# One more GpSimd DRAIN ahead of the last unit's scatter-adds in a mixture-of-experts layer

## The chip, the cores and the metric

The kernel runs on one core of a Trainium2 chip. The metric is the device time of one execution in microseconds (us), the median of several executions. A profile of one execution gives what each engine did: TensorE (PE, with its weight loads as PEld), VectorE (DVE), ScalarE (ACT), GpSimd (POOL) and SyncE (SP), and the 16 DMA engines.

## What is computed

A mixture-of-experts layer with a residual. 4096 tokens (64 x 64) of 256 values are normed and gated; each takes its two best of 8 experts. An expert is three dense layers, 256 to 512 to 512 to 256. The two results are weighted with the gate's values and added to the token's row.

```python
xn = rms_w * (x * jax.lax.rsqrt(var + EPS))
gate = xn @ wg_W + wg_b + (genre_embed @ gg_W + gg_b)
topk_w, topk_i = jax.lax.top_k(jax.nn.softmax(gate, axis=-1), TOP_K)
cw = jnp.sum(jax.nn.one_hot(topk_i, E) * topk_w[..., None], axis=-2)
h1 = jax.nn.relu(jnp.einsum('bsh,ehm->bsem', x, W1) + b1)
h2 = jax.nn.relu(jnp.einsum('bsem,emn->bsen', h1, W2) + b2)
out_e = jnp.einsum('bsen,enh->bseh', h2, W3) + b3
out = x + jnp.einsum('bseh,bse->bsh', out_e, cw)
```

The reference computes every expert for every token; the kernel computes only the two chosen ones.

## The kernel before

The kernel first gates all tokens and builds lists of tokens by expert, in tiles of 128 tokens. Tiles of one expert that follow each other form a unit of one to four tiles. The first 8 units (one tile for each expert) run while the rest of the routing is still computed. The other units come from a plan. How many of them there are, and how wide, depends on the data, so the program holds 40 plans, each as a branch of its own (a `Switch` at L1449); one of them runs. The units' order within a branch is fixed when the kernel is built: every engine gets its instructions in the order of the text.

For a unit, GpSimd gathers the tokens' rows and gate values with indirect DMAs (L844), SyncE passes the rows through a scratch in DRAM to turn them, ScalarE's queue brings the expert's weights, and TensorE does the three layers. In `step_fast` (L1296) the first two layers of a unit of two to four tiles are done by a scheme of seven products instead of eight (`Fast`); VectorE forms the sums. The third layer of a unit is done in the step of the unit behind it: `layer3(u - 1)` (L1147) and then `give(u - 1)` (L1156).

`give` is where a result leaves. For each tile VectorE forms `y` from the products in PSUM, the gate's weight and the bias (L1167), and GpSimd issues a scatter-add (L1168): an indirect DMA that adds the 128 rows of `y` to the tokens' rows of the output in DRAM. A token appears in two experts' units, and a row is read, added to and written back; so the scatter-adds of a unit wait until those of the unit before it have landed. Within a unit no token appears twice, and its scatter-adds don't wait for each other.

The steps of a branch are issued by `steps` (L1395), whose last argument, `last`, is the number of the plan's units and the head's 8. The step of unit `last - 1` is that of the last unit: it issues its first two layers and the scatter-adds of unit `last - 2`. One more step, `u == last`, issues the third layer of the last unit, tile by tile, and its scatter-adds (L1285 to L1289). Behind it the program ends: SyncE waits until all transfers have landed, every engine has a DRAIN, and all meet at a barrier. These instructions carry the line L1484.

In the run shown the last units have two tiles each. `steps` is also called with one unit at a time ahead of the branch (L1445); there `last` is far off.

Of the kernel before, what the change touches and what calls it, by code (L numbers as in the profile page):

```python
# [52 lines left out]
def kernel(  # L53
# [17 lines left out]
    nc = tc.nc  # L71
# [741 lines left out]
    def width(u):  # L813
        return BT if u < E else SQ * plan[u - E][1]

    def size(u):
        return (width(u) + BT - 1) // BT

    def paired(u):
        return size(u) > 1  # L820
# [49 lines left out]
    def gather_cw(u):  # L870
        for k, b in enumerate(tiles(u)):
            cg = cgs[b] = cgR[:, turn_of(u, k) % NCG]
            fetch(cg, (cwdA if b < E else cwdR)[:, :], b)
# [14 lines left out]
    def shuffle(u):  # L888

        nc.sync.dma_start(  # L890
            shs[:, slots(u)].rearrange("p s k f -> p s (k f)"),
            passing(u).rearrange("(s g) (b k) f -> (g b) s (k f)", g=P // SQ, b=SQ),
        )

    def transpose_x(u):
        bs, w, s0 = tiles(u), len(tiles(u)), slots(u).start
        if u > E:
            for k in range(w):
                V.transpose(  # L899
                    xT[:, :, s0 + k, :].rearrange("p c (b k) -> p k c b", b=SQ),  # L900
                    shs[:, s0 + k].rearrange("p k (a c) -> p k c a", a=SQ),
                )
            return
        if u < E:
            tps = [PB[4][:, c * BT : (c + 1) * BT] for c in range(HC)]
        else:
            tps = [PB[4], PB[7]]
        for c in range(HC):
            for k, b in enumerate(bs):
                g = ring(run, [P, H], "xg", 3, b) if u < E else xgR[u % 2][:, k]  # L910
                nc.tensor.transpose(tps[c][:, ts(k, BT)], g.rearrange("p (r c) -> p c r", c=HC)[:, c], ident)  # L911
            if u == E:
                (nc.scalar.copy if c else V.tensor_copy)(
                    xT[:, c, slots(u), :], tps[c].rearrange("p (s t) -> p s t", s=w)
                )
        if u < E:
            nc.scalar.copy(xT[:, :, s0, :], PB[4][:, 0 : HC * BT].rearrange("p (c t) -> p c t", c=HC))
# [35 lines left out]
    def stream_1(u, engine=mybir.EngineType.Activation):  # L953
        e = expert(u, engine)
        QUEUES[engine].dma_start(w1r[u % RING], W1[e].rearrange("e (p c) m -> p (e c) m", c=HC))

    def stream_3(u, engine=mybir.EngineType.Activation):
        e = expert(u, engine)
        QUEUES[engine].dma_start(w3r[u % RING], W3[e].rearrange("e (c p) h -> p (e c) h", p=P))

    def streams(u, end):
        if E < u + 2 < end:
            stream_1(u + 2)
        if E < u + 1 < end:
            stream_3(u + 1)

    def stage_1(u):

        if u < E:
            ww[u] = [w1r[u % RING], vT[:, :, u, :], w2a[:, u], w3r[u % RING]]  # L970
            return
        e = ex[u] = expert(u, mybir.EngineType.DVE)
        bb = ring(run, [P, 2, MC], "bb", 3, u)
        V.tensor_copy(bb.unsqueeze(2), vT[:, :, e])
        ww[u] = [w1r[u % RING], bb, st2, w3r[u % RING]]

    def stage_2(u):
        if u >= E:
            V.tensor_copy(st2, w2a[:, ex[u]].rearrange("p e c m -> p (e c) m"))

    def scales(u):

        for k, b in enumerate(tiles(u)):
            cw = ring(run, [P, 1], "cw", 8, turn_of(u, k))
            V.tensor_copy(cw, cgs[b][:, ex[u]])
            cgs[b] = cw

    def scaled(u, eng="V"):

        cws = []  # L990
        e = expert(u, mybir.EngineType.Activation) if eng == "A" and u >= E else ex.get(u)
        for k, b in enumerate(tiles(u)):
            cg = cgs.pop(b)
            bc = ring(run, [P, H], "bc", 4, turn_of(u, k))
            if u < E:
                cw, b3e = cg[:, u : u + 1], b3_sb[:, u, :]
            else:
                cw, b3e = cg, b3_sb[:, e].rearrange("p e h -> p (e h)")
            if eng == "V":
                V.tensor_scalar(bc, b3e, cw, None, ALU.mult)  # L1000
            else:
                nc.scalar.mul(bc, b3e, cw)
            cws.append((cw, bc))
        ex.pop(u, None)
        ww[u].append(cws)

    def layer1(u):
        w1, bb = ww[u][0:2]
        w = width(u)
        cols = xT[:, :, slots(u), :].rearrange("p c s t -> p c (s t)")  # L1010
        for m in range(MC):
            ph = PB[m][:, 0:w]
            for c in range(HC):
                nc.tensor.matmul(  # L1014
                    ph, lhsT=w1[:, c, ts(m, P)], rhs=cols[:, c, :], start=(c == 0), stop=(c == HC - 1)
                )
            nc.scalar.activation(hid[0][:, m, 0:w], ph, AF.Relu, bias=bb[:, 0, m : m + 1])

    def layer2(u, between=None):
        _, bb, w2 = ww[u][0:3]  # L1020
        for n in range(MC):
            ph = PB[n][:, 2 * BT : 3 * BT]
            for m in range(MC):
                nc.tensor.matmul(  # L1024
                    ph, lhsT=w2[:, m, ts(n, P)], rhs=hid[0][:, m, 0:BT], start=(m == 0), stop=(m == MC - 1)
                )
            nc.scalar.activation(hid[1][:, n, 0:BT], ph, AF.Relu, bias=bb[:, 1, n : n + 1])
            if between and n in between:
                between[n]()
# [117 lines left out]
    def layer3(u, which=None, order=range(MC)):  # L1147
        w3 = ww[u][3]
        for k in which or range(size(u)):
            for i, n in enumerate(order):  # L1150
                cols = within(u, k)
                nc.tensor.matmul(  # L1152
                    sums(u, k)[0 : cols.stop - cols.start], lhsT=hid[1][:, n, cols], rhs=w3[:, n, :], start=(i == 0), stop=(i == MC - 1)
                )
# [104 lines left out]
    def fetches_of(u, last):  # L1259
        far = E + 1 < u + 2 < last  # L1260
        if far:
            gather_unit(u + 2)
            stow(u + 2)
        return far

    def step(u, last):

        far = fetches_of(u, last)
        if u < last:
            layer1(u)  # L1270
            if u >= E:
                streams(u, last)
            stage_2(u)
        if u + 1 < last:
            gather_cw(u + 1)
        if u - 1 >= E:
            scales(u - 1)
        scaled(u - 1)
        if u + 1 < last:
            stage_1(u + 1)  # L1280
            if u + 1 > E:
                transpose_x(u + 1)
        if far:
            shuffle(u + 2)
        if u == last:  # L1285
            for k in reversed(range(size(u - 1))):
                layer3(u - 1, [k], (2, 3, 0, 1) if 2 * k * BT >= width(u - 1) else range(MC))
                give(u - 1, [k])
            return  # L1289
        layer3(u - 1)  # L1290
        if u == E - 1:
            stream_1(E + 2, mybir.EngineType.SP)
            stream_3(E + 1, mybir.EngineType.SP)
        give(u - 1)
# [100 lines left out]
    def steps(u0, u1, last):  # L1395
        for u in range(u0, u1):
            if u < last and paired(u):
                step_fast(u, last)
                continue
            step(u, last)  # L1400
            if u < last:
                layer2(u)

    CUT = E + NQT - 2
    ENGS = (
# [7 lines left out]
    with tc.manual_schedule():  # L1413
# [21 lines left out]
        for u in range(E - 1, CUT):  # L1435
            if u == CUT - 2:
                _, (arm,) = nc.values_load_multi_w_load_instructions(
                    nex[0:1, 0:1],
                    min_val=0,
                    max_val=len(ARMS) - 1,  # L1440
                    skip_runtime_bounds_check_because="the number of a shape of the tail",
                )
            elif u == CUT - 1:
                tc.switch_hint({e: arm for e in ENGS}, len(ARMS), "tail")
            steps(u, u + 1, E + NQT + 1)  # L1445
# [3 lines left out]
    for k in tc.Switch(arm, len(ARMS), hint="tail"):  # L1449
        for d, old in zip(kept, state):  # L1450
            d.clear()
            d.update({b: list(v) if isinstance(v, list) else v for b, v in old.items()})
        adds[:] = [list(a) for a in done]
        plan[:] = ARMS[k]
        last = E + len(plan)
        with tc.manual_schedule():
            steps(CUT, last + 1, last)
# [31 lines left out]
```

## Time and profile before

| what | us |
|---|---|
| median of 3 runs (465.6 to 468.07) | 467.16 |
| the profiled execution | 467.09 |
| its span, first to last instruction | 465.4 |
| TensorE busy | 450.8 (97%) |
| VectorE busy | 334.2 (72%) |
| GpSimd busy | 265.1 (57%) |
| ScalarE busy | 217.6 (47%) |
| transfers generated by GpSimd, share of 16 DMA engines | 22.2% |
| mean granted TensorE clock | 0.992 |

"Busy" counts the work of an engine and leaves out instructions that only steer it: moves of registers, branches, waits for semaphores and DRAINs. Such instructions appear in the views under a name with a q behind it (POOLq, SPq). An indirect DMA on GpSimd is busy while GpSimd generates its descriptors, and its data lands later. In the view in order of time a bracket gives how long the engine stood idle before the instruction and what ended that.

### The profile page before, as it was taken

How to read it: one execution, taken by the hardware profiler on the slowest of the kernel's cores; microseconds unless marked ns; L12 is line 12 of the kernel's file. 1: busy time of each engine (PE TensorE's matmuls, PEld its weight loads, DVE VectorE, ACT ScalarE, POOL GpSimd, SP SyncE). 2: the span in 40 equal slices, each digit the busy share in tenths (PEclk: the TensorE clock that was granted, in tenths of full speed). 3: DMA queues.
4: the chain of work that ended last, by engine and by line, in shares of the span. 5: the costliest groups of instructions: out<-in, count | busy, mean ns of one | idle time of the engine just before them, and what ended most of it. 6: DMA issues, size and time to landing. Idle time of an engine off the chain costs nothing.

```text
span 465.4 us, 8614 instructions
## 1 busy us (share of the span) xinstructions
PE 450.8 (97%) x2750; PEld 407.3 (88%) x2750; DVE 334.2 (72%) x889; ACT 217.6 (47%) x511; POOL 265.1 (57%) x231
## 2 busy tenths in 40 slices
PE   7899999999999999999999999999999999999991
PEld 5689999968888888888899999899999889999991
DVE  5787896266758576675867576777877887898850
ACT  4746443435344262526362625264464455555550
POOL 4255532757877878384746464757646545564222
PEclk9999999999999999999999999999999999999996
DMA  8699999793866766564636464655656664665322
GB/s 293 241 290 375 376 369 377 265 260 83 228 127 172 141 169 131 137 115 114 128 86 140 90 143 112 140 145 108 143 146 125 153 160 109 162 155 137 70 25 25
DMA packets 75629, 78.74 MB, mean 169 GB/s; under 512 B 34927, under 2 KB 64082, under 8 KB 75188
## 3 DMA queue, kind: packets, MB, share of 16 engines
q1 hardware_dynamic: 48976, 43.29, 30.1%
q0 software_dynamic: 14960, 17.47, 22.2%
q10 hardware_dynamic: 11636, 17.32, 11.3%
q8 instruction: 24, 0.39, 0.3%
q14 instruction: 33, 0.27, 0.2%
HBM read 62.60 MB, written 20.12 MB: 178 GB/s over the span
## 4 chain that ended last, share of the span: by engine, by line
PE 89%; issue 4%; DMA 3%; DVE 1%; POOL 1%; ACT 0%; ACTq 0%; DVEq 0%; POOLq 0%
PE pb L1105 50%; PE pb L1152 24%; PE pb L1024 6%; PE pb L1014 5%; DMA out_dram<-y,idxR 2%; PE pb L247 1%; POOL out_dram L1168 1%; PE pb L604 1%; PE pb L278 1%; DMA gTs<-in_L_cond_rms_w_dram 1%; PE pb L911 1%; DMA xg<-in_x_dram,idxA 1%; PE pb L284 0%; PE pb L539 0%; DVE hid L1123 0%
## 5 line engine op out<-in xcount | busy, mean ns | idle before, releaser
L1168 POOL DMA_INDIRECT out_dram<-y,idxR x59 | 95.4, 1618 | 105.0 <-DVE y L1167 52.4
L1152 PE MATMUL pb<-w3r,hid 128*128 128x256 f32 (+3 forms) x536 | 125.6, 380 | 0.0
L1152 PEld LDWEIGHTS pb<-w3r,hid 128*128 128x128 f32 (+3 forms) x536 | 96.9, 186 | 14.4 <-DVE y L1167 0.4
L1126 ACT ACTIVATE hid<-hid,bb 128x256 f32<-128x256 f32 (+13 forms) x148 | 70.2, 523 | 34.2 <-DVE hid L1123 30.2
L1105 PE MATMUL pb<-hid,big 128*128 128x256 f32 (+7 forms) x456 | 83.4, 326 | 0.0
L1105 PEld LDWEIGHTS pb<-hid,big 128*128 128x128 f32 x456 | 71.9, 191 | 5.9 <-issue 1.4
L844 POOL DMA_INDIRECT cg<-cwdR,idxR x59 | 63.9, 1083 | 18.0 <-issue 17.7
L1114 ACT COPY q1s<-pb 128x256 f32<-128x256 f32 (+7 forms) x54 | 25.3, 469 | 69.8 <-PE pb L1105 69.5
L1114 ACT COPY big<-pb 128x512 f32<-128x512 f32 (+7 forms) x57 | 27.2, 476 | 65.9 <-PE pb L1105 65.9
L1105 PE MATMUL pb<-mixB,big 128*128 128x256 f32 (+7 forms) x304 | 55.5, 326 | 0.1
L1105 PE MATMUL pb<-hotA,big 128*128 128x256 f32 (+7 forms) x304 | 52.3, 325 | 0.0
L1105 PEld LDWEIGHTS pb<-mixB,big 128*128 128x128 f32 x304 | 47.8, 191 | 3.1 <-DVE hid L1123 0.5
L1105 PEld LDWEIGHTS pb<-hotA,big 128*128 128x128 f32 x304 | 47.3, 191 | 2.7
L844 POOL DMA_INDIRECT xgE<-in_x_dram,idxR x31 | 33.5, 1082 | 17.3 <-issue 15.7
L1105 PE MATMUL pb<-mixX,iotx 128*128 128x128 f32 (+7 forms) x216 | 43.1, 322 | 0.0
L1105 PEld LDWEIGHTS pb<-mixX,iotx 128*128 128x128 f32 x216 | 35.5, 191 | 2.4
L844 POOL DMA_INDIRECT big<-in_x_dram,idxR x28 | 30.4, 1084 | 8.5 <-issue 7.0
L1167 DVE SCALAR_TENSOR_TENSOR y<-pb,cw,bc 128x256 f32<-128x256 f32 (+3 forms) x59 | 27.5, 479 | 7.7 <-PE pb L1152 7.2
L1126 ACT ACTIVATE hid<-pb,bb 128x128 f32<-128x128 f32 (+7 forms) x74 | 26.6, 411 | 12.4 <-PE pb L1105 12.1
L1024 PEld LDWEIGHTS pb<-hid,w2a 128*128 128x128 f32 x256 | 29.8, 192 | 1.1 <-issue 0.8
L1024 PE MATMUL pb<-hid,w2a 128*128 128x128 f32 x256 | 30.5, 276 | 0.0
L899 DVE STREAM_TRANSPOSE xT<-gTs 128x256 f32<-128x256 f32 x55 | 29.1, 638 | 0.0
(300 smaller groups left out, 643.1 us busy)
## 6 DMA issues: line engine op xcount, KB each, us to landing
w3r<-in_L_cond_W_dram ACTq DMA_DIRECT2D x17, 512.0 KB, 5.0
w2a<-in_L_cond_W_dram SPq DMA_DIRECT2D x8, 1024.0 KB, 13.3
w1r<-in_L_cond_W_dram ACTq DMA_DIRECT2D x16, 512.0 KB, 3.7
w1r<-in_L_cond_W_dram SPq DMA_DIRECT2D x11, 512.0 KB, 11.4
w3r<-in_L_cond_W_dram SPq DMA_DIRECT2D x10, 512.0 KB, 13.5
gTs<-scr SPq DMA_DIRECT2D x7, 512.0 KB, 4.2
out_dram<-in_x_dram SPq DMA_DIRECT2D x4, 768.0 KB, 9.3
big<-in_x_dram SPq DMA_DIRECT2D x4, 512.0 KB, 5.0
```

Source lines behind the costliest of these rows:

```text
L247: nc.tensor.transpose(TB[bank][:, ts(k, P)], xin[j][:, k, ts(c, P)], ident)
L278: nc.tensor.matmul(bank[r : r + 32, :], lhsT=wg_sb[:, c, :], rhs=turned(n), start=True, stop=True)
L844: return nc.gpsimd.indirect_dma_start(out=dst, out_offset=None, in_=src, in_offset=bass.IndirectOffsetOnAxis(ap=index(b), axis=0), bounds_ ...
L899: V.transpose(xT[:, :, s0 + k, :].rearrange("p c (b k) -> p k c b", b=SQ), shs[:, s0 + k].rearrange("p k (a c) -> p k c a", a=SQ),)
L1014: nc.tensor.matmul(ph, lhsT=w1[:, c, ts(m, P)], rhs=cols[:, c, :], start=(c == 0), stop=(c == HC - 1))
L1024: nc.tensor.matmul(ph, lhsT=w2[:, m, ts(n, P)], rhs=hid[0][:, m, 0:BT], start=(m == 0), stop=(m == MC - 1))
L1105: nc.tensor.matmul(bank[:, ts(n, self.w)], lhsT=w[:, c, ts(n, P)], rhs=x[:, c], start=new and n == 0 and c == 0, stop=n == HB - 1 and c == ...
L1114: nc.scalar.copy(self.q[(1, 6, 5).index(k)], self.tall(self.X if k == 5 else self.U))
L1126: nc.scalar.activation(out, src, AF.Relu, bias=ww[self.u][1][:, self.l, n : n + 1])
L1152: nc.tensor.matmul(sums(u, k)[0 : cols.stop - cols.start], lhsT=hid[1][:, n, cols], rhs=w3[:, n, :], start=(i == 0), stop=(i == MC - 1))
L1167: V.scalar_tensor_tensor(y[0:n], sums(u, k)[0:n], cw[0:n], bc[0:n], ALU.mult, ALU.add)
L1168: add = nc.gpsimd.indirect_dma_start(out=orows, out_offset=bass.IndirectOffsetOnAxis(ap=index(b)[0:n], axis=0), in_=y[0:n], in_offset=None ...
```

## The change

The loop of `steps` is written without its `continue`, and behind the step of unit `last - 1` GpSimd gets a DRAIN: an instruction that holds the engine's queue until the engine has finished what was issued before. It names no tile and waits for no semaphore. It stands behind the scatter-adds of unit `last - 2` and ahead of those of unit `last - 1`. Each of the 40 branches has one; of these one runs. The calls ahead of the branch never reach `u == last - 1`. Otherwise each engine's instructions and waits are the same and in the same order. Lines behind the edit are higher by two.

```diff
         for u in range(u0, u1):
             if u < last and paired(u):
                 step_fast(u, last)
-                continue
-            step(u, last)
-            if u < last:
-                layer2(u)
+            else:
+                step(u, last)
+                if u < last:
+                    layer2(u)
+            if u == last - 1:
+                nc.gpsimd.drain()
```

## The prediction

> **What bounds the kernel now.** I read the page from the top down and then went to its end, because the one added instruction can touch the end alone.
>
> ```profile
> span 465.4 us, 8614 instructions
> ...
> PE 450.8 (97%) x2750; PEld 407.3 (88%) x2750; DVE 334.2 (72%) x889; ACT 217.6 (47%) x511; POOL 265.1 (57%) x231
> ...
> L1168 POOL DMA_INDIRECT out_dram<-y,idxR x59 | 95.4, 1618 | 105.0 <-DVE y L1167 52.4
> ```
>
> TensorE is busy for 97% of the span, so it sets the pace up to its last matmul, shortly before 456 us. GpSimd (POOL) is not a bound in the middle: its scatter-adds stand 105 us idle, mostly waiting for VectorE's `y`. What lies behind TensorE's last matmul is a path of its own, and there a microsecond is a microsecond. The view in order of time, GpSimd's rows of its end:
>
> ```profile
> 445.40 1.55 POOL L1168 DMA_INDIRECT out_dram<-y,idxR  x1 [9.16 <-DVE y L1167]
> ...
> 447.26 1.55 POOL L1168 DMA_INDIRECT out_dram<-y,idxR  x1 [0.31 <-issue]
> ...
> 454.87 1.55 POOL L1168 DMA_INDIRECT out_dram<-y,idxR  x1 [6.06 <-DVE y L1167]
> ...
> 456.72 1.55 POOL L1168 DMA_INDIRECT out_dram<-y,idxR  x1 [0.30 <-issue]
> ```
>
> The first two are the scatter-adds of the last unit but one, issued in the step of the last unit; the other two are the last unit's own. The new DRAIN stands between the second and the third. There GpSimd does nothing from 447.26 + 1.55 = 448.81 to 454.87, which is the 6.06 us in the bracket.
>
> The page stops at 458.27 and the span at 465.4. Those 7.1 us are filled by instructions that it does not count as busy. The view of one source line shows them; L1484 is the end of the program (the four upper rows from the stretch 457.2 to 464.6, the last from 464.6 on; columns: minimum, median and maximum in ns, first and last start):
>
> ```profile
> L1484 SPq EVENT_SEMAPHORE  x10: 28/28/28, 458.8 to 460.9; - x10
> L1484 SPq DRAIN  x2: 7/10/13, 460.9 to 461.0; - x2
> L1484 POOLq DRAIN  x1: 7722/7722/7722, 456.8 to 456.8; - x1
> L1484 POOLq EVENT_SEMAPHORE  x1: 17/17/17, 464.6 to 464.6; - x1
> ...
> L1484 POOLq DRAIN  x2: 46/83/120, 464.7 to 465.1; - x2
> ```
>
> SyncE has seen every transfer land and stands at the barrier at 461.0. GpSimd reaches it only at 464.6, because its own DRAIN runs from 456.80 for 7.72 us, to 464.52. Every other engine's DRAIN is over by then. So the last 3.5 us of the path are GpSimd's DRAIN alone: 464.56 (the semaphore behind it) less 461.06 (SyncE's second DRAIN at 461.01, and 0.05 for the semaphore).
>
> How much of the 7.72 is waiting? The last scatter-add ends on GpSimd at 456.72 + 1.55 = 458.28, so 6.24 us come after it. In the chain of waits the second scatter-add lands 3.73 us after its start:
>
> ```profile
> 447.26 3.73 DMA out_dram<-y,idxR
> 450.98 0.03 issue
> 451.01 0.04 POOLq L1168
> ```
>
> By that the last one lands at 456.72 + 3.73 = 460.45, which agrees with SyncE's last waits at 458.8 to 460.9. The DRAIN goes on for 4.07 us after the last byte has landed. It is therefore not the landing alone that it waits for. The other DRAINs of the same engine are short:
>
> ```profile
> L1475 POOLq DRAIN  x1: 183/183/183, 0.4 to 0.4; - x1
> ```
>
> 183 ns at the start, before any transfer of GpSimd's, and 120 and 46 ns directly behind the long one. The long one is the first DRAIN behind all the transfers that GpSimd generates: 59 + 59 + 31 + 28 + 8 + 8 + 8 = 201 indirect ones by the groups of its engine, and 7 plain ones.
>
> **The change, part by part.** One DRAIN with no semaphore of its own, on one engine, in the branch of the program that runs. The order of all other instructions and their waits is the same. No transfer is added or moved, so SyncE's and ScalarE's queues see nothing. Queued behind it are only the wait for the two earlier scatter-adds (451.0) and the last unit's two scatter-adds; nobody but the end of the program waits for those. The rewritten `continue` is host code.
>
> *Price of the new DRAIN.* Before has no DRAIN in the middle. From below: 46 ns, the shortest of GpSimd's; from above 7.72 us, the whole long row, counted from 448.81. The nearest row is the long one, since it too stands behind some 200 transfers: 6.24 us after the scatter-add before it, or 6.24 x 206/208 = 6.18 if it goes by the number of transfers. I take 6.18: 448.81 + 6.18 = 454.99.
>
> *What is late next.* Behind the long DRAIN the next semaphore instruction came 0.04 us later, and a scatter-add that waits for nothing starts 0.30 us behind its predecessor (the bracket at 456.72). So the third scatter-add starts at 454.99 + 0.34 = 455.33 instead of 454.87: 0.46 us late. The fourth follows its predecessor and is as late: 457.18, ending at 458.74 and landing at 460.91. SyncE is at the barrier at 461.06 + 0.46 = 461.52.
>
> *Price of the last DRAIN.* From above: 6.24 us after 458.74, as before. From below: 0.05 us, as for the ones directly behind a DRAIN. If its length is what has piled up since the last DRAIN, two transfers are left of 208, 6.24 x 2/208 = 0.06 us, and even if it must also see them land it is over at about 460.95, before SyncE's 461.52. I take this.
>
> *Sum.* The barrier then falls to SyncE at 461.52 instead of GpSimd at 464.56: 3.04 us less. Against the profiled execution's own 467.09 us (span 465.36 and 1.73 around it) that is 464.05; the median of the runs shown, 467.16, is 0.07 above it: 464.1 us. The cover for the new DRAIN is the 6.06 us in which GpSimd waits for `y`; without it the DRAIN would cost its whole 6.2 and the change would lose about 3.
>
> The Trainium skill speaks against this. "VectorE: DVE Perf Modes", section "The DRAIN you can't avoid", says that the DRAINs of the program's start and end take about 12 ns, constantly, on all five engines. SyncE's rows (7 to 13 ns) agree and GpSimd's 7722 ns does not; by the page's price the new DRAIN would be free, the last one would have nothing to give, and the time would be 467.2. "Perfetto Trace Analysis", section "DMA Instruction — SWDGE (GPSIMD)", says that the profiled end of such a transfer is the end of descriptor generation, not of the data's movement. The 3.73 us to landing against 1.55 agree; if the DRAIN waited for movement alone, the last one would have ended near 460.5 and bounded nothing.
>
> **The rivals.**
>
> *Every DRAIN with a transfer behind the previous one pays the same* (a fixed round of questions to the 16 DMA engines, say). For it: the trace has just one such DRAIN, and the three short ones had no new transfer, so rows alone cannot separate "since the last DRAIN" from "any at all". Against it: 4.07 us after landing is long for a question whose answer is known. Then the new one ends at 448.81 + 6.24 = 455.05, or, counted from landing, 450.98 + 4.07 = 455.05 as well. The scatter-adds are 0.52 late and the last DRAIN adds its full 6.24: +0.5, 467.7 us. It begins to lose where the new DRAIN passes 454.87 - 0.34 - 448.81 = 5.72 us.
>
> *The long row belongs to the end of the program* and a DRAIN elsewhere takes 46 to 183 ns. Then it disappears in the gap and the time stays 467.2. For it: the line is the program's end, which holds more than this instruction. Against it: two other GpSimd DRAINs of the same line are short.
>
> *Slower: the new DRAIN is stretched by work beside it, and the last keeps its length.* The place is 448.9 to 454.8, where by the view of stretches VectorE is busy 2.47 us and ScalarE 2.44 of 5.90, while both are at 0.00 behind 458.3. The price goes by GpSimd's scatter-adds: 1552 ns at the quiet end, 2102 at the worst, a factor of 1.35. 6.24 x 1.35 = 8.4 us ends at 457.2, the scatter-adds are 2.7 late: 469.8 us. It passes 0.5% from a DRAIN of 5.72 + 2.34 = 8.06 us on. Against it: the median scatter-add, 1624, is only 1.05 times the quiet one, which gives 6.5 us and +0.8.
>
> **How the numbers follow.** What a measurement of this kernel can tell from no change is about 0.5%, 2.34 us: faster means under 464.8, slower over 469.5. The forecast gets 0.55. Its own range is 463.5 (the new DRAIN nearly free: 3.5 us less) to 465.2 (the new one somewhat longer than taken, or a last one that keeps half its 6.24, to 461.9, which leaves 2.7; with both about 2). I put 0.49 of the 0.55 under 464.8. The same price for every DRAIN gets 0.27, no effect 0.11, both within 0.5%; the stretched DRAIN gets 0.07, with 0.06 of it over 469.5. Faster 0.49, same 0.45, slower 0.06. The range for 8 in 10 has to hold most of the forecast and the two cases near 467: 463.4 to 468.0.
>
> **What would show it.** A GpSimd DRAIN of 5.5 to 6.5 us behind 448.8; the third scatter-add 0.3 to 0.6 us later than 454.87; the DRAIN at the end well under 3 us after its last scatter-add; and the barrier released by SyncE near 461.5. If the last DRAIN is again some 6 us, the first rival is right. If the one in the middle is under 0.2 and the last unchanged, it is the second. A DRAIN over 8 us in the middle is the third. The rows up to 448.8 should not differ at all; a difference there would be something that I have not seen.

## The result, and the profile after

| | before | changed |
|---|---|---|
| median of 22 runs each, us | 466.63 (465.17 to 470.26) | 464.39 (462.85 to 468.91) |
| ratio of the changed to before, 95% interval | | 0.9949 [0.9929, 0.9968] |
| the profiled execution, us | 467.09 | 463.89 |
| its span, us | 465.4 | 462.1 |

The change is 2.24 us faster by the medians, half a per cent, and the interval excludes no change. Here and below a ratio compares only the faster executions of the two kernels and a median takes all of them, so a ratio is not the quotient of two medians. The page of the changed kernel shows almost nothing of it:

```profile
span 462.1 us, 8615 instructions
...
PE 449.9 (97%) x2750; PEld 407.2 (88%) x2750; DVE 334.4 (72%) x889; ACT 217.5 (47%) x511; POOL 265.2 (57%) x231
...
L1168 POOL DMA_INDIRECT out_dram<-y,idxR x59 | 95.3, 1615 | 106.0 <-DVE y L1167 46.4
```

One instruction more, and every engine as busy as before to within 0.9 us. Only the idle time ahead of the scatter-adds has another cause in part: 46.4 us are put down to `y` instead of 52.4. The view in order of time says where. GpSimd's last four scatter-adds:

```profile
444.44 1.55 POOL L1168 DMA_INDIRECT out_dram<-y,idxR  x1 [9.16 <-DVE y L1167]
446.29 1.55 POOL L1168 DMA_INDIRECT out_dram<-y,idxR  x1 [0.30 <-issue]
455.01 1.55 POOL L1168 DMA_INDIRECT out_dram<-y,idxR  x1 [7.17 <-issue]
456.87 1.55 POOL L1168 DMA_INDIRECT out_dram<-y,idxR  x1 [0.31 <-issue]
```

The bracket of the third was 6.06 us, ended by `y`. Now it is 7.17, and `y` does not end it. VectorE's row for that `y`, before and then changed:

```profile
454.11 0.48 DVE L1167 SCALAR_TENSOR_TENSOR y<-pb,cw,bc 128x256 f32<-128x256 f32 x1 [1.49 <-PE pb L1152]
...
453.15 0.48 DVE L1167 SCALAR_TENSOR_TENSOR y<-pb,cw,bc 128x256 f32<-128x256 f32 x1 [1.49 <-PE pb L1152]
```

In the changed kernel it ends at 453.63, and the scatter-add starts 1.38 us later; before, it started 0.28 us after its `y` (454.59 to 454.87). So the DRAIN made it 1.10 us late. The views of the two lines L1404 (the new DRAIN) and L1486 (the end of the program, L1484 before), the latter from 455.5 to 461.3; columns are minimum, median and maximum in ns, then first and last start:

```profile
L1404 POOLq DRAIN  x1: 8894/8894/8894, 445.2 to 445.2; - x1
```

```profile
L1486 SPq EVENT_SEMAPHORE  x10: 28/28/28, 458.8 to 461.1; - x10
L1486 SPq DRAIN  x2: 7/10/13, 461.2 to 461.2; - x2
...
L1486 POOLq DRAIN  x1: 4893/4893/4893, 455.8 to 455.8; - x1
L1486 POOLq EVENT_SEMAPHORE  x1: 17/17/17, 461.3 to 461.3; - x1
```

The new DRAIN's row begins at 445.25, before the second scatter-add ahead of it has even started (446.29), so its length says little by itself; it has to be counted from that transfer's end. The new one lasts until 454.14, which is 6.30 us behind the end of the second scatter-add (447.85). The one at the end of the program ends at 460.73: 2.30 us behind the last scatter-add instead of 6.24. GpSimd is then at the barrier before SyncE, whose second DRAIN is at 461.2.

To compare executions, I count from the end of the third `y`, the last thing ahead of GpSimd's path, in the same trace:

| us after the third `y`'s end | before | changed |
|---|---|---|
| third scatter-add starts | 0.28 | 1.38 |
| fourth scatter-add ends | 3.69 | 4.79 |
| GpSimd's last long DRAIN ends | 9.93 | 7.10 |
| SyncE stands at the barrier | 6.42 | 7.61 |
| the span ends | 10.77 | 8.44 |

The tail, from the end of the third `y` to the end of the span, is 2.33 us shorter. The spans differ by 3.3 because `y` itself was 0.96 us earlier in this execution (453.63 against 454.59). The DRAIN cannot have caused that: the rows ahead of it were early already (the first scatter-add above at 444.44 instead of 445.40), and the medians' 2.24 us agree with the tail.

### The profile page after: what moved, and what is told of

Same layout as the page of the kernel before. It is cut to its first block, busy times and chain, and to the rows that moved or that the text cites. A ratio compares the mean times of both kernels' runs of the same rounds, so it can differ in the third digit from the quotient of the medians.

```text
span 462.1 us, 8615 instructions
## 1 busy us (share of the span) xinstructions
PE 449.9 (97%) x2750; PEld 407.2 (88%) x2750; DVE 334.4 (72%) x889; ACT 217.5 (47%) x511; POOL 265.2 (57%) x231
## 4 chain that ended last, share of the span: by engine, by line
PE 87%; DMA 5%; issue 3%; DVE 1%; POOLq 1%; POOL 0%; SPq 0%; ACT 0%; ACTq 0%; DVEq 0%
PE pb L1105 51%; PE pb L1152 23%; PE pb L1024 5%; PE pb L1014 4%; DMA w3r<-in_L_cond_W_dram 3%; PE pb L247 1%; DMA out_dram<-y,idxR 1%; PE pb L604 1%; DMA gTs<-in_L_cond_rms_w_dram 1%; PE pb L278 1%; DMA xg<-in_x_dram,idxA 1%; POOLq L1486 1%; PE pb L911 1%; POOL out_dram L1168 0%; PE pb L284 0%
## 5 line engine op out<-in xcount | busy, mean ns | idle before, releaser
L1168 POOL DMA_INDIRECT out_dram<-y,idxR x59 | 95.3, 1615 | 106.0 <-DVE y L1167 46.4
```

What stands on the lines that cost most here:

```text
L1168: add = nc.gpsimd.indirect_dma_start(out=orows, out_offset=bass.IndirectOffsetOnAxis(ap=index(b)[0:n], axis=0), in_=y[0:n], in_offset=None ...
```

## The experiments

Three things were open. Why is the long DRAIN long, and what does it count? What held the third scatter-add for 1.1 us? And is there a better place? The runs were made in three groups, each on one chip beside the kernel before, and the ratios are against the runs of that group. In the second and third group the executions were longer (before took 492.75 and 489.96 us) and scattered more, so their ratios are wide; there I rely on the tail in the traces, counted as above. It does not follow the length of the execution: 8.44 us in a span of 462.1 us and 8.48 in one of 481.7 for the changed kernel, 7.38 in 460.6 and 7.24 in 491.4 for the next one below. The profiles of these two groups show a lower granted clock (0.977 to 0.99), but that is not the whole reason: the changed kernel took 483.46 us at 0.99 in the third group and 464.46 at 0.994 in the first.

**The change again.** No edit; it is the yardstick for its group, and stands in the third group too.

> The changed kernel once more, on the chip of the three runs beside it. Both theories below: as on record, 2 to 2.5 us less than before (ratio about 0.995). DRAIN behind the scatter-adds of the last unit but one about 6.3 us behind the end of the scatter-add ahead of it, the next scatter-add 0.8 to 0.9 us behind its end and so about 1.1 us later than VectorE's y would allow; last DRAIN ends within 0.2 us of the landing of the last scatter-add.

Measured: 464.95 us, ratio 0.996 [0.9935, 0.9984], with the third scatter-add 1.31 us behind its `y` and a tail of 8.34.

> The changed kernel beside it on the same chip: from the end of the third y to the end of the span 8.3 to 8.5 us, 2.3 us less than before, ratio 0.995.

Measured: 485.49 us, ratio 0.9974 [0.9912, 1.0036], 1.40 and 8.48. The time by itself says nothing in this group; the tail repeats to 0.15 us over three executions.

**The DRAIN one step earlier.** It then stands in a longer gap.

```diff
-            if u == last - 1:
+            if u == last - 2:
                 nc.gpsimd.drain()
```

> The same DRAIN one step earlier, behind the step of unit last - 2, where GpSimd stood idle for 9.16 us before. Piled up (a DRAIN has to work off something for each transfer generated since the last DRAIN, some 20 to 30 ns each): 4 transfers are left for the last DRAIN, 0.1 us, hidden by their landing; the new one takes about 6.2 us and its restart 0.9, which is inside 9.16, so the last unit's scatter-adds are not late: 3.5 us less than before, ratio 0.9925, 1.1 us less than the changed kernel. First use (the first DRAIN behind any transfer is dear, later ones are not): the same. Every DRAIN pays the same: no gain. So this run tests the mis-sized term, the 1.1 us by which the scatter-adds are late, not the two theories against each other.

Measured: 462.33 us, ratio 0.9907 [0.9881, 0.9932]; the tail is 7.38 us. GpSimd's rows, the new DRAIN first, then the view in order of time, then the end of the program:

```profile
L1404 POOLq DRAIN  x1: 9072/9072/9072, 432.0 to 432.0; - x1
```

```profile
433.13 1.74 POOL L1168 DMA_INDIRECT out_dram<-y,idxR  x1 [0.31 <-DVE iotx L1075]
444.03 1.55 POOL L1168 DMA_INDIRECT out_dram<-y,idxR  x1 [9.16 <-DVE y L1167]
445.89 1.55 POOL L1168 DMA_INDIRECT out_dram<-y,idxR  x1 [0.30 <-issue]
453.51 1.55 POOL L1168 DMA_INDIRECT out_dram<-y,idxR  x1 [6.07 <-DVE y L1167]
```

```profile
L1486 SPq DRAIN  x2: 7/10/13, 459.7 to 459.8; - x2
...
L1486 POOLq DRAIN  x1: 3912/3912/3912, 455.4 to 455.4; - x1
```

The scatter-add ahead ends at 434.87 and the DRAIN at 441.1: 6.2 us again, in a gap that is 9.16 us long and is still ended by `y`. Both later gaps are as before (9.16 and 6.07), so nothing is late, and SyncE releases the barrier. This takes back the whole lateness and beats the change: the two intervals of this group, [0.9881, 0.9932] and [0.9935, 0.9984], do not meet. By the medians of the group it is 4.94 us less than before (467.27), though the tail accounts for 3.39 (10.77 - 7.38). Where the other 1.5 us come from is not shown: there are only six executions of it, and the group has no trace of before.

> The DRAIN one step earlier again, beside the two others on the same chip. 3.5 us less than before by its terms, ratio 0.9925; the first time gave 0.9907 with 0.9881 to 0.9932.

Measured: 488.62 us, ratio 0.9962 [0.9911, 1.0013], a tail of 7.24. The time is inconclusive; the tail is the same as in the first group within 0.14 us.

**The DRAIN at the start of the branch**, with far fewer transfers before it and far more to come.

```diff
-            if u == last - 1:
+            if u == CUT:
                 nc.gpsimd.drain()
```

> The one DRAIN behind the first step of the branch, when about a third of the 208 transfers have been generated. Piled up: the new one takes about a third of 6.2 us, 2 us, and the last one keeps what is left, about 4 us behind the last scatter-add instead of 6.24 (or 2.7 behind its landing instead of 4.07): 1.4 to 2.1 us less than before, ratio 0.9955 to 0.997. First use: the new one takes some 6 us, and the last one only waits for the landing: 3.5 us less, ratio 0.9925, unless the 6 us hold up the gathers behind it.

Measured: 463.23 us, ratio 0.9915 [0.9893, 0.9936], a tail of 7.28. The line of the new DRAIN:

```profile
L1404 POOLq DRAIN  x1: 10329/10329/10329, 177.8 to 177.8; - x1
```

Only 87 of GpSimd's transfers come before it, and yet it ends 7.45 us after the last of them, longer than the 6.24 us after 208. And the 121 transfers that follow cost the last DRAIN almost nothing: it ends 2.69 us after the last scatter-add, 0.56 us after SyncE has seen that land (461.34). A length in proportion to all transfers falls on both numbers. This was a miss for me as well: I had expected the last DRAIN to keep a good part of its length, and with it half of the gain at the end.

**What a DRAIN counts.** A kernel that computes none of the layers: SyncE copies `x` to the output, and GpSimd generates batches of transfers, waits until they have landed (a copy that reads the last of them), and drains.

```
for n in (2, 8, 32, 64):
    gathers(n)
    landed(n)
    nc.gpsimd.drain()
...
```

Behind these come 32 plain loads of 128 rows, 32 plain loads of one row of 32 bytes, 32 of SyncE's loads, 32 of GpSimd's copies, and twice 64 gathers with one DRAIN, each closed by a DRAIN.

> A kernel that computes none of the layers: it copies x to the output and measures DRAINs of GpSimd by themselves. Each batch is waited for until it has landed, by a copy on GpSimd, ahead of its DRAIN. Batches since the DRAIN before, in order: 0 transfers; 2, 8, 32, 64 gathers of 128 rows; 32 plain loads of 128 rows by GpSimd; 32 plain loads of one row of 32 bytes by GpSimd; 32 loads by SyncE; 32 copies on GpSimd and no transfer; 128 gathers; nothing. Piled up: 0.05 to 0.2 us for none, 0.1, 0.2 to 0.3, 0.6 to 1.0, 1.3 to 2.0 us for the gathers, 0.6 to 1.0 for the plain loads, 0.2 for SyncE's loads and for the copies, 2.6 to 4 us for 128. If it goes by descriptors and not by transfers, the loads of one row cost next to nothing. First use: some 4 to 6 us at the 2 gathers, and under 0.3 us at every one behind. Every DRAIN with a transfer behind the one before pays the same: about 4 us at 2, 8, 32, 64 and 128 alike.

Measured, in this order (the view of one line, stretch by stretch):

```profile
L49 POOLq DRAIN  x1: 447/447/447, 16.7 to 16.7; - x1
...
L49 POOLq DRAIN  x1: 939/939/939, 29.9 to 29.9; - x1
...
L49 POOLq DRAIN  x1: 2922/2922/2922, 75.0 to 75.0; - x1
...
L49 POOLq DRAIN  x1: 5591/5591/5591, 163.5 to 163.5; - x1
...
L53 POOLq DRAIN  x1: 2929/2929/2929, 188.6 to 188.6; - x1
L57 POOLq DRAIN  x1: 2924/2924/2924, 209.1 to 209.1; - x1
L61 POOLq DRAIN  x1: 319/319/319, 227.0 to 227.0; - x1
L64 POOLq DRAIN  x1: 373/373/373, 238.2 to 238.2; - x1
L69 POOLq DRAIN  x1: 2170/2170/2170, 410.0 to 410.0; - x1
```

All transfers have landed when these DRAINs begin, as the copy ahead of each waits for the last of them, so this is no waiting for data. The copy ahead of the fourth row:

```profile
163.56 0.28 POOL L38 COPY small<-rows 128x64 f32<-128x64 f32 x1 [1.78 <-DMA rows<-in_x_dram,idx]
```

From 2 to 64 transfers it is a straight line: (5591 - 447) / 62 = 83 ns for each, where I had expected 20 to 30. The rows begin just ahead of the copy's start and so contain it. Counted from the copy's end the DRAINs take 250 ns behind 2 transfers and 5296 behind 64: 81 ns for each, on a line that begins at about 0.09 us. It does not matter whether they are gathers or plain loads, nor how large: 2929 ns for 32 loads of 128 rows of 1 KB, 2924 for 32 of one 32-byte row. SyncE's loads and GpSimd's own computing add nothing (319, 373). What counts is the number of transfers that GpSimd has generated since its last DRAIN. The first four rows refute two theories: that every DRAIN pays the same once a transfer has come since the last one, and that only the first DRAIN is dear. The last row is the surprise: 128 transfers cost less than 32.

**The same over more counts**, to see where the line breaks: 48, 80, 96, 104, 112, 120, 128, 160, 208 and 16 gathers, one DRAIN behind each.

> The measuring kernel again (it computes none of the layers and copies x to the output), gathers alone, each batch landed before its DRAIN: 48, 80, 96, 104, 112, 120, 128, 160, 208 and 16 transfers since the DRAIN before. The first measuring run gave 0.08 us and 0.083 us for each transfer up to 64, but 1.88 us behind its copy for 128, as if 22 were left. Sawtooth (a store of about 106 that starts anew when it is full): 4.1, 6.7, 8.0, 8.7 us for 48, 80, 96, 104, then 0.6, 1.2, 1.9, 4.6, 8.5 for 112, 120, 128, 160, 208, and 1.4 for 16. Worked off in idle moments once it is large: about 1.9 for everything from 112 on. Straight: 9.4, 10, 10.7, 13.4, 17.3.

Measured, all ns: 4272, 6907, 8204, 8857, 9511, then 1506, 2547, 2360, 6274, and 1589 for the 16. Four of the rows, for 112, 120, 160 and 208:

```profile
L49 POOLq DRAIN  x1: 9511/9511/9511, 618.4 to 618.4; - x1
...
L49 POOLq DRAIN  x1: 1506/1506/1506, 786.5 to 786.5; - x1
...
L49 POOLq DRAIN  x1: 2360/2360/2360, 1189.0 to 1189.0; - x1
...
L49 POOLq DRAIN  x1: 6274/6274/6274, 1487.2 to 1487.2; - x1
```

The straight line holds up to 112 (9511 - 5591 over 48 is 82 ns for each) and breaks before 120. By that slope, some 14 transfers are left to work off at 120, 28 at 160 and 75 at 208. So the earlier ones seem to drop out once enough have piled up; but 160 - 28 and 208 - 75 give 132 and 133 dropped where 120 - 14 gives 106, and 128 gives 98 here and 106 in the first measuring kernel, so it is not a plain count that wraps. None of the three theories that I had written down fits all rows.

The rows behind 120 are not quite like the others. From 855 us on, in the batch of 128, to the end of the batch of 208 GpSimd's MOVEs took some 700 ns instead of 29. The transfers of the batches of 160 and 208 came mostly 1.4 us apart instead of 1.3, and the DRAINs behind 128, 160 and 208 began 1.2 to 2.4 us after the copy's end. In the batches of 120 and 128 no pause is seen among the transfers. In both those of 160 and 208 there is one ahead of the 114th transfer, about where the line breaks; in the batch of 160:

```profile
1115.52 1.00 POOL L28 DMA_INDIRECT rows<-in_x_dram,idx  x1 [0.40 <-issue]
1119.50 1.00 POOL L28 DMA_INDIRECT rows<-in_x_dram,idx  x1 [2.98 <-issue]
```

Whether the earlier transfers are worked off there, and where it happens at 120, stays open. The straight part does explain the branch's start: 87 is on it (0.09 + 87 x 0.081 = 7.1 us, measured 7.45), and 121 is just past the break, where little is left. And 208 in the kernel before gives 6.24 us behind its last scatter-add, close to the 6274 ns of the 208 here, though that batch was issued at another pace.

**A DRAIN in each of two steps**, the change's and the one before it.

```diff
-            if u == last - 1:
+            if last - 2 <= u < last:
                 nc.gpsimd.drain()
```

> The DRAIN one step earlier and the one of the change, both. The first takes about 6.2 us in its 9.16 us, the second has 2 transfers behind it and only waits for their landing, about 2.3 us, of the 6.06 us idle; the last scatter-adds start 0.28 us behind VectorE's y as in before. So the DRAIN of the change costs nothing when there is nothing left for it: the time of the DRAIN one step earlier, ratio 0.99 to 0.9925, and 1 us less than the changed kernel.

Measured: 489.09 us, ratio 0.9956 [0.9914, 0.9997], a tail of 7.21. The two new DRAINs:

```profile
L1404 POOLq DRAIN  x2: 4965/6944/8923, 454.9 to 467.8; - x2
```

The first ends 6.06 us behind the scatter-add ahead of it. The second, in the very place of the change, ends 2.37 behind, which is little more than the landing (2.24 us behind the end of the scatter-add there in the trace of the change), and the third scatter-add then starts 0.28 us behind its `y`. So it is not the place that made the change's DRAIN long.

> Both DRAINs again on another chip. From the end of the third y to the end of the span 7.2 to 7.4 us (10.77 in before, 8.44 in the changed kernel): 3.4 us less than before, ratio 0.9925, and 1 us less than the changed kernel.

Measured: 486.76 us, ratio 0.9968 [0.986, 1.0076], a tail of 7.40. The time is inconclusive.

**A DRAIN in every step of the branch.**

```diff
-            if u == last - 1:
+            if CUT <= u < last:
                 nc.gpsimd.drain()
```

> A DRAIN behind every step of the branch that runs, some 14 of them. Piled up: the first takes 7.4 us as in the run with it alone, the others 0.083 us for each of the 4 to 16 transfers since the one before, 0.4 to 1.4 us, or the landing of the last of them, some 2.3 us, whichever is later; the last one as short as with the DRAIN one step earlier. Where the 2.3 and a restart of 0.9 fit into GpSimd's idle stretch of each step (3.67 us and more in the steps of before), the time is that of the DRAIN one step earlier, ratio 0.99 to 0.9925; where they do not, the gathers of the steps with four tiles come later and it may be 1 to 3 us more. First use: the first dear, the others the landing alone.

Measured: 490.06 us, ratio 0.9954 [0.9885, 1.0023], a tail of 7.30.

```profile
L1404 POOLq DRAIN  x16: 3602/5871/10697, 198.0 to 473.0; - x16
```

The first ends 7.82 us behind the transfer ahead, the others 1.9 to 4.6, the last ones 2.15 to 2.35. The tail is no shorter than with one DRAIN a step earlier, so there is nothing left for it to gain.

**The DRAIN behind the last scatter-adds**, so that the end's own DRAIN comes second.

```diff
-            if u == last - 1:
+            if u == last:
                 nc.gpsimd.drain()
```

> A control for the place: the one DRAIN stands behind the last unit's scatter-adds, where nothing covers it. Piled up: it takes the 6.24 us that the last one took, from the end of the last scatter-add, and the DRAIN of the program's end behind it is short: from the end of the third y to the end of the span 10.8 to 10.9 us as in before, ratio 1.000. If an extra DRAIN helped wherever it stands, this would be near 0.995 too.

Measured: 491.4 us, ratio 1.0028 [0.9964, 1.0092]; by time no difference can be told, but the tail is 11.43 us, 0.66 longer than before.

```profile
L1404 POOLq DRAIN  x1: 8238/8238/8238, 481.4 to 481.4; - x1
```

```profile
L1486 POOLq DRAIN  x3: 34/114/121, 490.1 to 490.8; - x3
```

The long DRAIN has moved to the branch's line, 6.32 us behind the last scatter-add, and the end of the program has only short ones. So the length belongs to the transfers and not to the end of the program, and with no gap to lie in the DRAIN saves nothing. I had put this case near no change. The 0.66 is mostly what was hidden beside the long DRAIN and now comes behind it: 0.46 us from its end at 489.67 to the next one at 490.13.

## Why the prediction was right, and the term that was not

464.1 was predicted, 464.39 measured. Step by step:

- *The bound at the end.* Right: the barrier waited for GpSimd's DRAIN alone. With it shortened, SyncE releases the barrier, as in the forecast.
- *The price of the new DRAIN*, 6.18 us behind the scatter-add ahead: 6.30. The reason given, that it works off what has piled up since the last DRAIN, is shown by the measuring kernels. The formula beside it, in proportion to all transfers (0.03 us each), is wrong: it is 0.083 us each up to 112 transfers, and 120 cost less than 32. It did no harm because 206 is next to the 208 that were measured, which was luck; for 87 it would have given 2.6 us instead of 7.45.
- *The price of the last DRAIN*: over before SyncE is ready. Right: 460.73, half a microsecond before SyncE's second DRAIN. With two transfers left it waits for little but the landing.
- *The restart of the third scatter-add* was mis-sized: "the third scatter-add starts at 454.99 + 0.34", that is 0.46 us late. It starts 0.87 us behind the DRAIN, in the change and in both repeats, and so, with 6.30 + 0.87 against the 6.06 us of the gap, about 1.1 us late. The chain of waits of the changed kernel (start, us, engine) shows what lies between:

```profile
447.85 6.33 issue
454.18 0.03 POOLq L1168
454.21 0.05 issue
454.25 0.04 POOLq L1168
454.30 0.49 issue
454.79 0.03 POOLq L1168
454.82 0.19 issue
455.01 0.43 POOL out_dram L1168
```

Behind the DRAIN (454.14) come a MOVE, the semaphore that the prediction counted (454.25; in the kernel before it stood at 451.01, under the wait for `y`), and then 0.49 us that show no instruction. In the second measuring kernel a gather also starts only 0.80 us after the end of the DRAIN ahead (behind the 112, for one). I take the 0.49 us for the sequencer's handling of the transfer, which no row shows by itself. My 0.30 came from a scatter-add right behind another, where this handling can lie under the transfer ahead. In the kernel before it would lie under the wait for `y`, so that a scatter-add could start 0.28 us behind `y`. While the DRAIN runs, GpSimd's sequencer shows no other instruction, so the time comes after it. In the sum, 0.12 more of DRAIN and 0.53 more of restart make 0.65 us; the forecast was 3.04 and the tail shows 2.33, which is 0.71 apart. With the DRAIN a step earlier the lateness is gone and the tail gives 10.77 - 7.38 = 3.39, near the 3.5 named as the most there was to gain.

- *The rivals.* The same price for every DRAIN needed 6 us at the end and would have given 467.7: the last took 2.30. The end-of-program theory needed a DRAIN under 0.2 us in the middle: it took 6.30, and the DRAIN behind the last scatter-adds moved the length with it. The stretched DRAIN needed over 8 us: not here.
- *Rows ahead of 448.8* "should not differ at all": they did, by 0.96 us. I had not allowed for the difference between two executions, which would have passed for an effect if only the spans had been compared.

That the time came out closer than the working is luck: the median before, over 22 runs, lay at 466.63, below the 467.16 of three runs that the sum began from, which made up for most of the 0.7 us that the sum gave too much. A slip in the forecast's own range changed nothing: 3.5 us less than 467.16 is 463.7, not 463.5.

## What to carry to other kernels

Look at what stands behind the last busy instruction, in the views that show the instructions which steer: a DRAIN on an engine that generates transfers can be the longest thing on that path, and it must be counted from the end of the transfer ahead of it. Here such a DRAIN cost 0.083 us for each transfer generated since the last one, whatever its size, up to 112 transfers, and 6.1 to 6.3 us behind the 204 to 208 of this layer. So an earlier one takes that cost off the end if it lies in an idle stretch that holds it and the restart (6.3 + 0.9 us here: the 9.16 us gap hid it, the 6.06 us gap did not). Take the price of a restart behind a hold from a place where the queue was really held, not from two instructions that follow each other.

## What the hardware showed unexpectedly

- The price of a DRAIN rises with the number of transfers up to 112 (9511 ns) and falls to 1506 ns at 120; at 208 it is 6274. Why it falls, and by what rule, is open.
- In the measuring kernels all of this is paid although every transfer has landed, and 32 bytes cost as much as 128 KB (2924 and 2929 ns for 32 of them).
- Behind a DRAIN the next scatter-add starts 0.87 us after its end, with 0.49 us that show no instruction; in the kernel before it starts 0.28 us after the data that it waits for.
